# Offset and mask projections in 64x64 TensorE tiles, and convolution statistics as ScalarE sums, in a four-layer convolution kernel

## The chip, the cores and the metric

One core of a Trainium2 chip runs the whole program as one launch. The metric is device microseconds from start to end of that launch, lower being better. The core has five engines that run their own instruction streams side by side: TensorE (PE, matrix multiplies into PSUM), VectorE (DVE), ScalarE (ACT), GpSimd (POOL) and SyncE (SP, which here only issues DMAs). PE has a second row in the profile, PEld, for loading the stationary operand of a multiply. All data is float32, and each float32 matrix multiply of the program appears as two MATMUL instructions in the profile.

## The reference

The input x is 8 images of 128 channels and 96x96 pixels. Four residual layers follow each other, each preceded by a group normalization. Only layer 0 is touched by the change:

```python
x1 = lax.conv_general_dilated(x, dw_w, window_strides=(1, 1), padding=[(1, 1), (1, 1)], feature_group_count=C, ...)
x1 = x1 + dw_b[None, :, None, None]
mu = jnp.mean(x1, axis=(1, 2, 3), keepdims=True)
var = jnp.var(x1, axis=(1, 2, 3), keepdims=True)
x1 = (x1 - mu) * lax.rsqrt(var + GN_EPS)
x1 = x1 * gn_w[None, :, None, None] + gn_b[None, :, None, None]
x1 = jax.nn.gelu(x1, approximate=False)
om = jnp.einsum('nhwc,oc->nhwo', jnp.transpose(x1, (0, 2, 3, 1)), om_w) + om_b
...
offs = om[..., :2 * K2].reshape(N, H, W, G, K2, 2)
mask = om[..., 2 * K2:]
...
samp = gather(y0i, x0i) * ((1 - ly) * (1 - lx))[..., None] + gather(y0i, x0i + 1) * ((1 - ly) * lx)[..., None] + ...
out = jnp.sum(samp * mask[..., None], axis=4)
...
x = x + _L0_conv_ref(_gn(x), ...)
x = x + _L1_conv_ref(_gn(x), L1_conv_kernel)
x = x + _L2_conv_ref(_gn(x), L2_conv_weight, L2_conv_alpha_x, L2_conv_alpha_w)
x = x + _L3_conv_ref(_gn(x), L3_conv_kernel, L3_conv_bias)
```

Layer 0 is a deformable convolution. A depthwise 3x3 convolution, normalized over the whole image and passed through GELU, is projected by a 128-channel matrix onto 216 values for each pixel: a horizontal offset, a vertical offset and a mask for each of 72 taps (8 groups of 9). The image is then sampled bilinearly at the displaced places.

## The kernel before

The program has three stages in time: layer 0, then layers 1 and 2 together, then layer 3. Layer 0 works on chunks. An image is split into two bands of 48 rows, and chunk c of 12 holds four rows of each band, so 96 chunks in all. Two layouts are in use. In the plain layout a partition is one of 128 channels, and the free axis holds the two bands (2 x 384). In the band layout a partition is a band and one of 64 channels, and the free axis holds the two halves of the channels (2 x 384). The normalized image `xq` is in band layout.

For each image, `image` computes the statistics and the normalization, and then the depthwise convolution: nine taps for each chunk (`tap`, L568), each of four 64x64 multiplies whose stationary operands are diagonal matrices. Its input is in band layout and its result in plain layout. ACT moves the result out of PSUM (L588), DVE takes statistics with two `bn_stats` (L596), and SP stores it to DRAM as `x1d`. For the first image only, four of the twelve chunks are convolved by DVE (L560, L562) with the result in band layout. At the end of an image `bn_aggr` (L628), `mid1` and `end1` make the scale and bias of the following GELU.

`chunk` then does the sampling. SP loads the stored convolution in plain layout (L655), ACT applies GELU (L660), and `project` (L666) makes the three projections, vertical, mask and horizontal, each as two 128x128 multiplies with 384 columns. ACT turns the offsets into tent weights h (L679, L669, L692), DVE multiplies the mask in (L721), POOL multiplies vertical by horizontal weights to `wt` (L764, nine per chunk). For each of 25 shifts PE selects and sums the taps (`select`, L774, four 64x64 multiplies), and DVE multiplies the selected weights by the shifted image (L791). The 25 products of a chunk are added up by one of three engines, as a letter for each says: P by POOL (L809), D by DVE (L798), E by PE as four multiplies with an identity (L751). ACT moves the sum out (L817) and SP stores it (L820).

PSUM has three buffers `w` for the selects, projections, convolutions and small statistics, and one buffer `s` for the sums. There are three `wt` buffers and five `pr` buffers for products.

The order of instructions is fixed when the program is built. `Plan` is given tasks with an engine, a cost, dependencies, buffers and a priority, and steps through them: a free engine takes the ready task of lowest priority value whose buffers are free. The constants `STEP`, `OM_SLOT`, `WT_AHEAD`, `ADD_LAG`, `DW_SLOT` and `DW_PACE` make the priorities. The costs only set the order; on the chip the engines wait for each other by semaphores.

Of the kernel before, what the change touches and what calls it, by code (L numbers as in the profile page):

```python
# [11 lines left out]
F32 = mybir.dt.float32  # L12
I32 = mybir.dt.int32
AF = mybir.ActivationFunctionType
# [53 lines left out]
ADDERS = ("PPEDEPEPEPPDEEPEDPEDPEPPD", "PPPEEDPEPPEDDEEPPPEDEEPED")  # L68
LAST_ADDERS = "EDEPPEEDPEEDPEEEDPPEPEEPD"
# [5 lines left out]
WT_AHEAD = 6.3  # L75
ADD_LAG = 660.8
DW_SLOT = 2.2
DW_PACE = 1.1
# [122 lines left out]
def kernel(  # L201
# [35 lines left out]
    def half(j):  # L237
        return slice(j * HC, (j + 1) * HC)
# [154 lines left out]
    with ExitStack() as ph:  # L393
# [7 lines left out]
        omq = wp.tile([P, 3, P], F32, name="omq")  # L401
# [5 lines left out]
        dwbq = wp.tile([P, NB], F32, name="dwbq")  # L407
        for j in range(NB):
            rows = slice(j * HC, j * HC + GR)
            taps = slice(j * GR, (j + 1) * GR)  # L410
            nc.scalar.dma_start(sel[rows, :, :], c_sel[taps, :, half(j)])
            nc.scalar.dma_start(shift[rows, :], c_shift[taps, :])
            with nc.allow_non_contiguous_dma(reason="216 biases, one per partition"):
                nc.scalar.dma_start(omb[rows, :], om_b[:, taps].rearrange("k r -> r k"))
            for k in range(3):
                nc.scalar.dma_start(omq[:, k, rows], om_wT[:, k * GK + j * GR : k * GK + (j + 1) * GR])
            nc.scalar.dma_start(dwq[half(j), :, :], dw_w.rearrange("(j c) t -> c j t", c=HC))
            with nc.allow_non_contiguous_dma(reason="128 biases"):
                nc.scalar.dma_start(dwbq[half(j), :], dw_b.rearrange("(j c) o -> c (j o)", c=HC))
        dwd = wp.tile([P, NB, K2, HC], F32, name="dwd")  # L420
# [13 lines left out]
        for name, n, psum in (  # L434
            ("w", 3, True), ("s", 1, True), ("pr", 5, False), ("acc", 2, False), ("acc2", 2, False),
            ("y", 2, False), ("wt", 3, False), ("h0", 2 * NR, False), ("h1", 2 * NR, False),
            ("o", 2, False), ("x1c", 2, False), ("x1", 2, False), ("junk", 1, False),
        ):
            if psum:
                tiles = [pp.tile([P, CB, 512], F32, name=f"ps_{name}{k}") for k in range(n)]  # L440
            else:
                tiles = [wp.tile([P, NB, FB], F32, name=f"{name}_{k}") for k in range(n)]
            plan.pool(name, tiles, in_order=name != "w")
# [19 lines left out]
        for i in range(2):  # L463
            smalls.append({
                name: wp.tile([P, n], F32, name=f"{name}{i}")
                for name, n in (
                    ("st", NB * NST * 6), ("mv", 2 * NB), ("mean", NB), ("d", NB), ("sd", NB), ("sc", NB), ("bi", NB),
                    ("st1", NST * NB * 6), ("mv1", 2), ("mean1", 1), ("v1", 1), ("sd1", 1), ("sc1", 1), ("bi1", 1),
# [3 lines left out]
        def image(i, at):  # L472
# [73 lines left out]
            st1 = small["st1"][:].rearrange("p (a b) -> p a b", b=6)  # L546
            outs, stats1 = [], []
            for c in range(NST):
# [28 lines left out]
                for t in range(K2):  # L577
# [5 lines left out]
                    else:  # L583
# [4 lines left out]
                    lambda x1=x1, ps=ps, bias=None if on_dve else dwb[:]: nc.scalar.activation(  # L588
                        x1.tile[:], ps.tile[:, :, :FB], AF.Identity, **({} if bias is None else {"bias": bias})
# [3 lines left out]
                for b in range(NB):  # L593
                    stats1.append(plan.task(
                        "DVE", 0.49,
                        lambda b=b, c=c, x1=x1: nc.vector.bn_stats(st1[:, c * NB + b, :], x1.tile[:, b, :]),  # L596
                        [ev], when + 8, uses=[x1],
                    ))
# [47 lines left out]
            t = plan.task("DVE", 0.7, lambda: end1(b4.tile), [t], when, uses=[b4])  # L646
# [3 lines left out]
        def chunk(i, c, at, made):  # L650
# [3 lines left out]
            ld = plan.task(  # L654
                "SP", 0.64, lambda: nc.sync.dma_start(x1.tile[:], band_rows(x1d[i], c)),  # L655
                [outs[c]], at - STEP - 10, uses=[x1], lag=3.0,
            )
            ge = plan.task(
                "ACT", 0.95,
                lambda: nc.scalar.activation(x1.tile[:], x1.tile[:], AF.Gelu, bias=bi1[:], scale=sc1[:]),  # L660
                [ld, coefs1], at - STEP, uses=[x1],
            )

            def project(k, ps):
                for b in range(NB):
                    nc.tensor.matmul(ps[:, b, :FB], omq[:, k, :], x1.tile[:, b, :], start=True, stop=True)  # L666
# [6 lines left out]
            for k in (1, 0):  # L673
                ps, o = plan.buf("w"), plan.buf("o")
                when = at - STEP + (0.5 if k == 1 else OM_SLOT)
                t = plan.task("PE", 1.6, lambda k=k, ps=ps: project(k, ps.tile), [ge], when, uses=[ps, x1, o])
# [33 lines left out]
                if k == 1:  # L710
                    pm = plan.buf("w")
                    t = plan.task(
                        "PE", 1.6, lambda pm=pm: project(2, pm.tile),
# [107 lines left out]

        neg1 = wp.tile([P, 1], F32, name="neg1")
# [827 lines left out]
```

## Time and profile before

| | us |
|---|---|
| three runs | 5731.64, 5794.74, 5796.0 |
| their median | 5794.74 |
| profiled execution, its own time | 5726.59 |
| its span, first to last instruction | 5724.6 |
| first and last select of layer 0 (L774) | 142.7 and 3507.8 |
| first multiply of layer 1 (L1157) | 3562.1 |
| first multiply of layer 3 (L1561) | 4964.2 |
| mean granted TensorE clock | 0.988 of full |

The first number of a row in a view of windows is the stretch in us from the start of the span, then its length, and for each engine the time it was busy in it and, in brackets, the instructions that began in it. In a timeline a row has the start, the length, the engine, the line of the source, the operation, output and inputs, and how many instructions were merged into the row. In a row of a group the mean of one instruction is in ns after the total in us; after the bar stands the idle time of the engine just before those instructions, and what ended most of it. The three runs and the profiled execution lie at two places, near 5730 and near 5795.

### The profile page before, as it was taken

The page shows a single profiled execution, that of the slowest core. Times are in us where ns is not written, and L with a number is a line of the kernel's source. Part 1 is how long each engine was busy: PE and PEld are TensorE (multiplying, and loading weights), DVE is VectorE, ACT ScalarE, POOL GpSimd, SP SyncE. Part 2 cuts the span into 40 slices and gives each one's busy share as a digit, 9 for nine tenths or more (in the row PEclk, how much of TensorE's full clock was granted, in tenths as well). Part 3 has the DMA queues.
Part 4 walks back from the last instruction along what each step waited for, and adds up shares of the span by engine and source line. Part 5 has one row for each costly group of instructions (what it writes and reads, how often), then busy time and mean ns, then how long its engine had stood idle before and what let it go on. Part 6 is the DMA issues. An engine that isn't in the chain of part 4 may idle for free. (4 is left out here: it accounts for less than half of the span.)

```text
span 5724.6 us, 121348 instructions
## 1 busy us (share of the span) xinstructions
PE 5466.1 (95%) x49697; PEld 2948.3 (52%) x49697; DVE 4982.4 (87%) x7139; ACT 3131.3 (55%) x4141; POOL 4535.9 (79%) x2830
## 2 busy tenths in 40 slices
PE   4999999999999999999999996999999999899999
PEld 2444444444444444444444443544444444599999
DVE  6889889889889889889888997789999988788887
ACT  3655555555555655655655552467877776533333
POOL 0999999999999999999999996699999998322222
PEclk9999999999999999999999998999999999999999
DMA  5111111211211211211111113323333321233232
GB/s 123 50 57 57 55 57 57 57 57 57 58 57 57 58 57 57 55 59 57 48 48 46 43 40 88 104 76 87 95 96 98 90 65 48 75 105 102 98 111 78
DMA packets 434625, 397.81 MB, mean 69 GB/s; under 512 B 248976, under 2 KB 421520, under 8 KB 434064
## 3 DMA queue, kind: packets, MB, share of 16 engines
q1 hardware_dynamic: 403872, 351.23, 21.7%
q10 hardware_dynamic: 30192, 38.75, 1.9%
q8 instruction: 395, 6.47, 0.5%
q14 instruction: 166, 1.36, 0.1%
HBM read 238.90 MB, written 150.99 MB: 68 GB/s over the span
## 5 line engine op out<-in xcount | busy, mean ns | idle before, releaser
L774 PE MATMUL ps_w<-wt,sel 64*64 64x384 f32 x19200 | 1850.8, 488 | 47.1 <-ACT x L588 14.3
L791 DVE TENSOR_TENSOR pr<-ps_w,xq 128x768 f32<-128x768 f32 x1824 | 1675.3, 949 | 252.5 <-PE ps_w L774 201.9
L809 POOL TENSOR_TENSOR acc<-acc,pr 128x768 f32<-128x768 f32 x882 | 1614.0, 1837 | 194.8 <-DVE pr L791 193.3
L764 POOL TENSOR_TENSOR wt<-h,h 128x768 f32<-128x768 f32 x864 | 1578.0, 1837 | 191.3 <-ACT h L692 137.7
L774 PEld LDWEIGHTS ps_w<-wt,sel 64*64 64x64 f32 x19200 | 698.9, 132 | 967.5 <-issue 475.2
L1157 PE MATMUL ps_C<-dC,km 128*128 128x384 f32 x2304 | 768.3, 490 | 21.1 <-POOL dC L1145 9.6
L751 PE MATMUL ps_s<-pr,idq 64*64 64x384 f32 x7536 | 754.6, 484 | 0.4 <-ACT y L817 0.4
L679 ACT ACTIVATE o<-ps_w,omb 128x768 f32<-128x768 f32 x192 | 172.8, 900 | 1022.6 <-PE ps_w L666 948.3
L1285 DVE SCALAR_TENSOR_TENSOR ps_C<-xqC,w2s,ps_C 128x768 f32<-128x768 f32 x660 | 664.8, 1012 | 22.3 <-POOL xqC L1247 11.3
L1501 POOL TENSOR_TENSOR xtD<-xtD,cr 128x384 f32<-128x384 f32 x192 | 192.1, 1001 | 601.7 <-ACT cr L1500 601.7
L568 PE MATMUL ps_w<-xq,dwd 64*64 64x384 f32 x6624 | 630.4, 488 | 13.5 <-ACT x L588 10.3
L1157 PEld LDWEIGHTS ps_C<-dC,km 128*128 128x128 f32 x2304 | 429.3, 189 | 358.4 <-issue 38.6
L669 ACT ACTIVATE h<-o,shift 128x768 f32<-128x768 f32 x576 | 533.0, 925 | 12.2 <-ACT o L679 0.7
L791 DVE TENSOR_TENSOR ps_w<-ps_w,xq 128x768 f32<-128x768 f32 x480 | 458.8, 956 | 50.3 <-PE ps_w L774 50.1
L692 ACT ACTIVATE h<-h 128x768 f32<-128x768 f32 x576 | 486.3, 844 | 17.5
L666 PE MATMUL ps_w<-x1c,omq 128*128 128x384 f32 x1152 | 450.3, 514 | 16.6 <-DVE pr L791 11.3
L1302 POOL TENSOR_TENSOR ptC<-ptC,ptC 128x768 f32<-128x768 f32 x252 | 464.8, 1845 | 0.2
L798 DVE TENSOR_TENSOR acc<-ps_w,acc 128x768 f32<-128x768 f32 x480 | 455.7, 949 | 6.0
L751 PEld LDWEIGHTS ps_s<-pr,idq 64*64 64x64 f32 x7536 | 292.5, 133 | 313.7 <-issue 268.4
L1145 POOL TENSOR_TENSOR dC<-ywC 128x392 f32<-128x392 f32 x384 | 359.9, 972 | 98.3 <-PE ps_C L1157 53.6
L1561 PE MATMUL ps_b<-tr,km 128*128 128x192 f32 x2304 | 407.5, 325 | 14.4 <-DVE tr L1546 14.4
L568 PEld LDWEIGHTS ps_w<-xq,dwd 64*64 64x64 f32 x6624 | 258.2, 133 | 302.2 <-issue 229.7
(180 smaller groups left out, 7087.3 us busy)
## 6 DMA issues: line engine op xcount, KB each, us to landing
ywC<-y SPq DMA_DIRECT2D x80, 480.0 KB, 3.9
x1c<-x1d SPq DMA_DIRECT2D x96, 384.0 KB, 3.6
acc<-in_x SPq DMA_DIRECT2D x192, 192.0 KB, 3.3
y<-y SPq DMA_DIRECT2D x96, 384.0 KB, 3.2
ysC<-y SPq DMA_DIRECT2D x96, 384.0 KB, 3.3
x<-oC SPq DMA_DIRECT2D x192, 192.0 KB, 2.7
xtD<-x SPq DMA_DIRECT2D x24, 1536.0 KB, 7.1
out<-xtD ACTq DMA_DIRECT2D x24, 1536.0 KB, 5.7
```

Source lines behind the costliest of these rows:

```text
L568: nc.tensor.matmul(ps.tile[half(j), b, :FB], dwd[half(b), j, t, :], xq[half(b), r0 : r0 + RB, j, c0 : c0 + W], start=(t == 0), stop=(t == ...
L669: nc.scalar.activation(h, o, AF.Abs, bias=shift[:, k * NR + r : k * NR + r + 1])
L692: lambda h=h: nc.scalar.activation(h.tile[:], h.tile[:], AF.Relu, bias=1.0, scale=-1.0),
L751: nc.tensor.matmul(total.tile[half(j), b, :FB], idq[half(b), :], pr.tile[half(b), j, :], start=first, stop=last)
L764: lambda wt=wt, hy=hy, hx=hx: nc.gpsimd.tensor_tensor(wt.tile[:], hy.tile[:], hx.tile[:], ALU.mult),
L774: nc.tensor.matmul(ps.tile[half(b), j, :FB], sel[half(j), n, :], wt.tile[half(j), b, :], start=True, stop=True)
L791: nc.vector.tensor_tensor(view(pr.tile), view(ps.tile), x_s, ALU.mult)
L798: lambda ps=ps: nc.vector.tensor_tensor(acc.tile[:], ps.tile[:, :, :FB], acc.tile[:], ALU.add),
L809: lambda pr=pr, acc2=acc2: nc.gpsimd.tensor_tensor(acc2.tile[:], acc2.tile[:], pr.tile[:], ALU.add),
L1157: nc.tensor.matmul(ps.tile[:, b, :FB], km1[:, k, x_, :], d.tile[:, k, :, x_ : x_ + W], start=(x_ == 0), stop=(x_ == 2))
L1285: nc.vector.scalar_tensor_tensor(view, rows8(src, t), w[:, t : t + 1], view, ALU.mult, ALU.add)
L1302: lambda a=parts[0], b=pt: nc.gpsimd.tensor_tensor(a.tile[:], a.tile[:], b.tile[:], ALU.add),
```

## The change

The input of the projections is now loaded in band layout. The projection weights `omq` are arranged for 64x64 tiles, and each of the three projections is eight 64x64 multiplies, two accumulating steps over the halves of the channels with four tiles each. GELU needs a scale and bias for each half of the channels and becomes two activations of 384 columns. The load is two DMAs of 64 partitions in place of one of 128.

The statistics of the convolution come from ACT: the activation that moves the result out of PSUM also gives the sum, and a second activation squares the difference from the bias and gives its sum. Both `bn_stats` go. At the end of an image five small DVE operations take the place of `bn_aggr`, and `end1` makes a scale and a bias for both halves.

Setup loads `omq` in eight DMAs in place of six, and two vectors more, in two DMAs each. Some letters of the adders trade places: the two patterns in turn keep their counts (11 P, 9 E, 5 D and 10 P, 10 E, 5 D), and that of the last image goes from 8 P, 12 E, 5 D to 7 P, 13 E, 5 D. Four constants of the priorities and the costs given to the planner change. Layers 1 to 3 are not touched.

```diff
-ADDERS = ("PPEDEPEPEPPDEEPEDPEDPEPPD", "PPPEEDPEPPEDDEEPPPEDEEPED")
-LAST_ADDERS = "EDEPPEEDPEEDPEEEDPPEPEEPD"
+ADDERS = ("PPEDEPEPEPPDEEPDEPEDPEPPD", "PPPEEDPEPPEDDEEEPPEDPEPED")
+LAST_ADDERS = "EDEEEEPDPEEDPEEEDPPEPEPED"
...
-WT_AHEAD = 6.3
-ADD_LAG = 660.8
-DW_SLOT = 2.2
-DW_PACE = 1.1
+WT_AHEAD = 6.45
+ADD_LAG = 1048.6
+DW_SLOT = 2.21
+DW_PACE = 4.76
...
-        omq = wp.tile([P, 3, P], F32, name="omq")
+        omq = wp.tile([P, NB, 3, P], F32, name="omq")
...
-            for k in range(3):
-                nc.scalar.dma_start(omq[:, k, rows], om_wT[:, k * GK + j * GR : k * GK + (j + 1) * GR])
+            for b in range(NB):
+                for m in range(NB):
+                    nc.scalar.dma_start(
+                        omq[half(b), j, :, m * HC : m * HC + GR],
+                        om_wT[half(j), :].rearrange("c (k r) -> c k r", k=3)[:, :, m * GR : (m + 1) * GR],
+                    )
...
+                nc.scalar.dma_start(gnwq[half(j), :], gn_w.rearrange("(j c) o -> c (j o)", c=HC))
+                nc.scalar.dma_start(gnbq[half(j), :], gn_b.rearrange("(j c) o -> c (j o)", c=HC))
...
                     "ACT", 0.9,
-                    lambda x1=x1, ps=ps, bias=None if on_dve else dwb[:]: nc.scalar.activation(
-                        x1.tile[:], ps.tile[:, :, :FB], AF.Identity, **({} if bias is None else {"bias": bias})
+                    lambda c=c, x1=x1, ps=ps, bias=None if on_dve else dwb[:]: nc.scalar.activation(
+                        x1.tile[:], ps.tile[:, :, :FB], AF.Identity, **({} if bias is None else {"bias": bias}),
+                        accum_out=st1[:, 0, c : c + 1],
                     ),
                     prev, when + 6, uses=[ps, x1],
                 )
-                for b in range(NB):
-                    stats1.append(plan.task(
-                        "DVE", 0.49,
-                        lambda b=b, c=c, x1=x1: nc.vector.bn_stats(st1[:, c * NB + b, :], x1.tile[:, b, :]),
-                        [ev], when + 8, uses=[x1],
-                    ))
+                jk = plan.buf("junk")
+                stats1.append(plan.task(
+                    "ACT", 0.9,
+                    lambda c=c, x1=x1, jk=jk: nc.scalar.activation(
+                        jk.tile[:], x1.tile[:], AF.Square, bias=ndwb[:], accum_out=st1[:, 1, c : c + 1]
+                    ),
+                    [ev], when + 8, uses=[x1, jk],
+                ))
...
-                nc.vector.tensor_scalar(r, r, gnw[:], None, ALU.mult)
-                nc.vector.tensor_copy(sc1[:], r)
-                nc.vector.tensor_scalar(r, r, mean1[:], -1.0, ALU.mult, ALU.mult)
-                nc.vector.tensor_scalar(bi1[:], r, gnb[:], None, ALU.add)
+                for j in range(NB):
+                    q = ps[:, 1, 1 + j : 2 + j]
+                    nc.vector.tensor_scalar(q, r, gnwq[:, j : j + 1], None, ALU.mult)
+                    nc.vector.tensor_copy(sc1[:, j : j + 1], q)
+                    nc.vector.tensor_scalar(q, q, mean1[:], -1.0, ALU.mult, ALU.mult)
+                    nc.vector.tensor_scalar(bi1[:, j : j + 1], q, gnbq[:, j : j + 1], None, ALU.add)
...
-            t = plan.task(
-                "DVE", 0.8, lambda: nc.vector.bn_aggr(mv1[:], small["st1"][:]), stats1, when
-            )
+            def aggr1():
+
+                d1, n = small["d1"], NST * NB * FB
+                nc.vector.tensor_reduce(d1[:], st1, AX.X, ALU.add)
+                nc.vector.tensor_scalar(mv1[:], d1[:], 1.0 / n, None, ALU.mult)
+                nc.vector.tensor_scalar(d1[:, 0:1], mv1[:, 0:1], dwb[:], None, ALU.subtract)
+                nc.vector.tensor_scalar(d1[:, 1:2], d1[:, 0:1], d1[:, 0:1], -1.0, ALU.mult, ALU.mult)
+                nc.vector.tensor_scalar(mv1[:, 1:2], mv1[:, 1:2], d1[:, 1:2], None, ALU.add)
+
+            t = plan.task("DVE", 0.8, aggr1, stats1, when)
...
-                "SP", 0.64, lambda: nc.sync.dma_start(x1.tile[:], band_rows(x1d[i], c)),
+            def load_x1():
+                for b in range(NB):
+                    f0 = b * HB * W + c * FB
+                    nc.sync.dma_start(
+                        x1.tile[half(b), :, :], x1d[i].rearrange("(j c) f -> c j f", c=HC)[:, :, f0 : f0 + FB]
+                    )
...
-                lambda: nc.scalar.activation(x1.tile[:], x1.tile[:], AF.Gelu, bias=bi1[:], scale=sc1[:]),
+            def gelu():
+                for j in range(NB):
+                    rows = x1.tile[:, j, :]
+                    nc.scalar.activation(rows, rows, AF.Gelu, bias=bi1[:, j : j + 1], scale=sc1[:, j : j + 1])
...
             def project(k, ps):
-                for b in range(NB):
-                    nc.tensor.matmul(ps[:, b, :FB], omq[:, k, :], x1.tile[:, b, :], start=True, stop=True)
+
+                for j in range(NB):
+                    for m in range(NB):
+                        for b in range(NB):
+                            nc.tensor.matmul(
+                                ps[half(m), b, :FB],
+                                omq[half(b), j, k, half(m)],
+                                x1.tile[half(b), j, :],
+                                start=(j == 0),
+                                stop=(j == NB - 1),
+                            )
...
-                t = plan.task("PE", 1.6, lambda k=k, ps=ps: project(k, ps.tile), [ge], when, uses=[ps, x1, o])
+                t = plan.task("PE", 1.29, lambda k=k, ps=ps: project(k, ps.tile), [ge], when, uses=[ps, x1, o])
```

More of the change, by code (lines that the diff above doesn't have):

```diff
@@ L407 @@
         dwbq = wp.tile([P, NB], F32, name="dwbq")
+        gnwq = wp.tile([P, NB], F32, name="gnwq")
+        gnbq = wp.tile([P, NB], F32, name="gnbq")
         for j in range(NB):
@@ L414 @@
                 nc.scalar.dma_start(omb[rows, :], om_b[:, taps].rearrange("k r -> r k"))
-            for k in range(3):
-                nc.scalar.dma_start(omq[:, k, rows], om_wT[:, k * GK + j * GR : k * GK + (j + 1) * GR])
+            for b in range(NB):
[4 more added lines that the diff above has]
+                    )
             nc.scalar.dma_start(dwq[half(j), :, :], dw_w.rearrange("(j c) t -> c j t", c=HC))
-            with nc.allow_non_contiguous_dma(reason="128 biases"):
+            with nc.allow_non_contiguous_dma(reason="128 values of each"):
                 nc.scalar.dma_start(dwbq[half(j), :], dw_b.rearrange("(j c) o -> c (j o)", c=HC))
+                nc.scalar.dma_start(gnwq[half(j), :], gn_w.rearrange("(j c) o -> c (j o)", c=HC))
+                nc.scalar.dma_start(gnbq[half(j), :], gn_b.rearrange("(j c) o -> c (j o)", c=HC))
         dwd = wp.tile([P, NB, K2, HC], F32, name="dwd")
@@ L442 @@
                 tiles = [wp.tile([P, NB, FB], F32, name=f"{name}_{k}") for k in range(n)]
-            plan.pool(name, tiles, in_order=name != "w")
+            plan.pool(name, tiles, in_order=name not in ("w", "junk"))
         def load_rows(i, lo, hi):
@@ L467 @@
                     ("st", NB * NST * 6), ("mv", 2 * NB), ("mean", NB), ("d", NB), ("sd", NB), ("sc", NB), ("bi", NB),
-                    ("st1", NST * NB * 6), ("mv1", 2), ("mean1", 1), ("v1", 1), ("sd1", 1), ("sc1", 1), ("bi1", 1),
+                    ("st1", 2 * NST), ("mv1", 2), ("d1", 2), ("mean1", 1), ("v1", 1), ("sd1", 1), ("sc1", NB), ("bi1", NB),
                 )
@@ L544, in image @@
                 ))
-            st1 = small["st1"][:].rearrange("p (a b) -> p a b", b=6)
+            st1 = small["st1"][:].rearrange("p (k c) -> p k c", k=2)
             outs, stats1 = [], []
@@ L645, in image @@
             )
-            t = plan.task("DVE", 0.7, lambda: end1(b4.tile), [t], when, uses=[b4])
+            t = plan.task("DVE", 1.2, lambda: end1(b4.tile), [t], when, uses=[b4])
             return outs, t, sc1, bi1
@@ L653, in chunk @@
             x1 = plan.buf("x1c")
-            ld = plan.task(
-                "SP", 0.64, lambda: nc.sync.dma_start(x1.tile[:], band_rows(x1d[i], c)),
[L656 to L662, printed above, removed]
-            def project(k, ps):
-                for b in range(NB):
-                    nc.tensor.matmul(ps[:, b, :FB], omq[:, k, :], x1.tile[:, b, :], start=True, stop=True)
+            def load_x1():
[8 more added lines that the diff above has]
+                    nc.scalar.activation(rows, rows, AF.Gelu, bias=bi1[:, j : j + 1], scale=sc1[:, j : j + 1])
+            ld = plan.task("SP", 1.2, load_x1, [outs[c]], at - STEP - 10, uses=[x1], lag=3.0)
+            ge = plan.task("ACT", 1.15, gelu, [ld, coefs1], at - STEP, uses=[x1])
+            def project(k, ps):
+                for j in range(NB):
[8 more added lines that the diff above has]
+                            )
             def absolute(h, o, k, r):
@@ L712, in chunk @@
                     t = plan.task(
-                        "PE", 1.6, lambda pm=pm: project(2, pm.tile),
+                        "PE", 1.29, lambda pm=pm: project(2, pm.tile),
                         [ge] + [tent[1, r][0] for r in RES_ORDER], when + 5, uses=[pm, x1],
@@ L820, in chunk @@
             plan.task("SP", 0.56, lambda: nc.sync.dma_start(band_rows(y1[i], c), y.tile[:]), [ev], at + STEP, uses=[y], lag=2.5)
+        ndwb = wp.tile([P, 1], F32, name="ndwb")
+        nc.vector.tensor_scalar(ndwb[:], dwb[:], -1.0, None, ALU.mult)
         neg1 = wp.tile([P, 1], F32, name="neg1")
```

## The prediction

> **What bounds the kernel now.** I read the page first: its busy shares, the slices and the chain that ended last. The chain goes back only to 3521.78 us, where the loads of layers 1 and 2 begin; layer 0 ends before that, so the stage the change touches must be read from its own windows.
>
> ```profile
> PE   4999999999999999999999996999999999899999
> DVE  6889889889889889889888997789999988788887
> POOL 0999999999999999999999996699999998322222
> ```
>
> Up to slice 24 (3.4 ms) PE and POOL are both at nine tenths and DVE close behind. The small dips of DVE repeat, once for each image. So I cut one image into windows. The sum of a chunk leaves ACT (L817) at 1048, 1378 and 1479 us after nine and three more chunks; the other images repeat this to within 2 us. The third row is the last image.
>
> ```profile
> core 0: us, PE busy (x) PEld busy (x) DVE busy (x) ACT busy (x) POOL busy (x), PEclk, DMA share, GB/s
> 1048.00:1378.00 330.00, 326.32 (x3560) 147.84 (x3556) 287.39 (x341) 169.41 (x219) 299.09 (x168) 1.00 0.19 57
> 1378.00:1479.00 101.00, 95.36 (x984) 41.16 (x980) 95.02 (x127) 70.11 (x95) 98.12 (x56) 1.00 0.21 56
> 3187.00:3512.00 325.00, 323.18 (x3488) 143.59 (x3484) 313.32 (x354) 164.52 (x212) 307.84 (x172) 1.00 0.12 36
> ```
>
> The reader is to see two regimes. In nine chunks of twelve, while PE also makes the next image's convolution, PE is busy 98.9% and POOL 90.6%: PE sets the pace. In the other three there is no convolution, POOL is busy 97.1% and PE 94.4%: POOL sets the pace. In the last image PE (99.4%), DVE (96.4%) and POOL (94.7%) are close together.
>
> **The change part by part.** *Projections, 57 us gained.* The timeline of PE shows one among 64x64 work:
>
> ```profile
> 163.81 2.14 PE L774 MATMUL ps_w<-wt,sel 64*64 64x384 f32 x24
> 165.75 1.50 PE L751 MATMUL ps_s<-pr,idq 64*64 64x384 f32 x16
> ...
> 173.14 0.82 PE L774 MATMUL ps_w<-wt,sel 64*64 64x384 f32 x8
> 173.89 1.56 PE L666 MATMUL ps_w<-x1c,omq 128*128 128x384 f32 x4
> 175.38 0.88 PE L774 MATMUL ps_w<-wt,sel 64*64 64x384 f32 x8
> ```
>
> Starts count, as lengths overlap. Eight 64x64 instructions take (165.75-163.81)/3 = 0.647 us. From 173.14 to 175.38 are 2.24 us for eight of them and one projection, which so costs 1.59: 1.49 of its own and 0.10 before it can start. As 16 instructions of 64x64 it will cost 2 x 0.647 = 1.29. Gain 0.30.
>
> Here two statements of the Trainium skill meet this row. "TensorEngine Tiling (Array Packing)", section The Problem, has the full array underused where a dimension is at most 64. These projections contract 128 channels into 108 columns: by that rule there is nothing to gain, and the sum would lose these 57 us. Its Key Properties say that a change of tiling mode drains the array; by that only the 0.10 goes, 0.10 x 3 x 63 = 19 us. The rows decide: beyond the entry, four full-array instructions take 1.49 us against 1.29 for sixteen small ones with the same multiplications. Accumulating twice into one bank is covered by the convolution, which adds nine taps in 64x64 tiles (L568, 488 ns mean, as L774's 488).
>
> It counts only where PE sets the pace: 27 projections in nine chunks, seven images, 7 x 27 x 0.30 = 57 us. POOL and DVE allow it: 330-8 leaves POOL at 299/322 = 93%, below the 97% it reaches elsewhere. In the POOL-bound three chunks I count nothing, since the adders keep their counts: 0, with bounds of 10 us either way for the altered order.
>
> *Statistics off DVE, 14 us gained.* These rows price them and what replaces them:
>
> ```profile
> L596 DVE BATCH_NORM_STATS2 st<-x 128x6 f32<-128x384 f32 x192 | 100.4, 549 | 22.6 <-ACT x L588 22.6
> L705 ACT ACTIVATE junk<-junk,neg 128x768 f32<-128x768 f32 x192 | 179.5, 935 | 5.6
> L705 ACT ACTIVATION_READ_ACCUMULATOR junk<-junk,neg 128x1 f32 x192 | 35.9, 187 | 0.0
> L537 ACT ACTIVATE xq<-xq,bi,sc 128x384 f32<-128x384 f32 x192 | 121.4, 698 | 0.1
> L660 ACT ACTIVATE x1c<-x1c,bi,sc 128x768 f32<-128x768 f32 x96 | 96.7, 1015 | 0.2
> POOL wt L764 <- DVE st L596: 18.2, 6, 3.3
> PEld ps_w L666 <- DVE st L596: 8.4, 14, 0.6
> ```
>
> DVE loses 24 x 0.549 = 12.6 us in the nine chunks of an image, where it is not the limit. Only waits that ended with it count: 18.2 + 8.4 us in all. I take about half, 2 us an image, 14; ends 0 and 30.
>
> *More on ACT, nothing.* A convolution chunk adds a Square with its accumulator read (935+187 ns, as L705) and one more read, 1.3 us; GELU in halves adds 2 x 0.70 - 1.01 = 0.4. No table load is added in the built instruction order. ACT goes from 169 of 330 us to about 188 of 322 (12 x 1.3 + 9 x 0.4 more), 58%: its idle time covers it. Uncovered it would be 96 x 1.7 = 163 us. Queued behind a Square are the moves of projections out of PSUM (L679), for which PE's next buffer waits.
>
> *Small operations at an image's end.* Five reductions and scalings for one `bn_aggr` (0.8 us) and four more in `end1` add some 1.3 us on DVE by the 0.2 to 0.28 us of such operations; they fall in the POOL-bound three chunks, with DVE at 94%. I leave them inside that part's bounds.
>
> *DMAs.* The split load adds one issue, 0.7 us by the two of the residual (1.29) against one of 0.56, on SP. Behind it stand loads of the next image and the store of y. "DMA: Bandwidth & Descriptors", Rules for kernel authors, calls halves in two DMAs not worth it, as both use the same engines. By that rule it is pure cost, at most 96 x 0.7 = 67 us if every issue were late. The rows price less: 192 KB of the residual land in 3.3 us, 384 KB of x1 in 3.6, DMA engines are at 19%, and SP issues some 6 us in 36. Nothing. The six added setup issues on ACT's queue (0.34 to 0.7 us each, 3 us) end near 26 us, before ACT's first work at 47.9; the statistics of x, still loading until 42, cover them. Uncovered: 3 us.
>
> *Start, 13 us gained.* From 50 to 117 us DVE is busy 62.1 us, of which 22 `bn_stats` of L596 are 10.9, and the convolution by DVE makes PE wait. Against it the tail grows: Square and read (1.1) for a `bn_stats` (0.55), 1.3 us of small operations, GELU halves, and normalizations that the new order puts before the first GELU. I take 5 us, ends 0 and 10. The new order also puts two of the second image's convolution chunks (18 taps, 11.6 us) before the first select, into idle time of PE:
>
> ```profile
> 127.21 7.94 PE L666 MATMUL ps_w<-x1c,omq 128*128 128x384 f32 x16 [4.41 <-ACT x1c L660]
> 142.69 6.08 PE L774 MATMUL ps_w<-wt,sel 64*64 64x384 f32 x48 [7.54 <-POOL wt L764]
> ```
>
> That relieves PE in the first chunks until POOL limits them: 8 us, ends 4 and 11. How long a convolution holds one of three PSUM buffers is unaltered, though `DW_PACE` grows: on average 4.8 selects stand between its first and last tap, 5.0 before.
>
> *Last image, 3 us gained.* PE loses 0.90 and takes one more addition (0.65) a chunk, POOL one fewer. DVE at 96.4% is late next: 3, ends 0 and 8.
>
> **Sum:** 57+14+13+3 = 87 us in layer 0; the other layers stay.
>
> **Against which time.** The sum is made in an execution of 5726.59 us (span 5724.6). The median of the runs is 5794.74, 68 higher: of four known executions two lie near 5730, two near 5795, and the trace does not show why. I set the forecast between, 5761 - 87 = 5674 us; on the lower level it is 5640, on the upper 5708.
>
> **The rivals.** *Waits take it.* With PE quicker, POOL's products and DVE's releases of PSUM become late in the nine chunks also; 30 us remain, mostly the start: 5731. For: three engines near 90% with three buffers each. Against: POOL stands at 90.6% there and has shown 97%.
>
> *Stalls go too.* Shorter projections hold PSUM less long and DVE is freer, so PE's waits (L666 alone waits 98.3 us for DVE products, on its weight row) shrink, and the POOL-bound part gains: 140 us, 5621. For: the planner's cost for a projection now equals the chip's. Against: in those chunks PE idles only 3.7 of 330 us.
>
> *Slower: ACT comes late.* If the Square stands before the move of a projection, PE lacks a buffer. At 1.7 us a chunk fully exposed, 163 - 87 = 76 us slower: 5837; it decides from 55% exposure. For: ACT moves all PSUM results but the products. Against: ACT idles 49% there, and PE's waits for L588 sum to tens of us only. Slower by 2% needs about 2.1 us of new waits a chunk.
>
> *It doesn't do what it says:* four tiles that run one after another would need over 2.6 us a projection. The rows of L568 exclude it.
>
> **How the numbers follow.** Chances: the sum above 62%, own range of gain 60 to 115; stalls too 20%; waits take it 13%; ACT late 5%. 2% is 116 us from the median, so 5679, about what a measurement of this kernel can tell from no change. The first case passes that on the lower level (half of 62%) and with 4% on the upper, the second nearly always (20%): faster 0.55. The rest is within 2%, 0.42, and slower keeps 0.03. The range: the second case on the lower level gives 5587 and the third on the upper 5765; leaving out a tenth at either end, 5600 to 5738.
>
> **What would show it.** Projections of 1.29 us from start to start with no entry gap; the nine chunks near 320 us with PE at 98%, the three still near 100 with POOL at 97%; first select near 137; ACT below 60%. Wrong would be PE below 96% in the nine chunks, or waits of PE for L679 or the Square of more than 50 us.

## The result and the profile after

The changed kernel's median is 5703.81 us (20 runs, 5697.09 to 5769.25) against 5794.97 for the kernel before on the same chip (20 runs, 5725.57 to 5797.87). The ratio is 0.9887 with a 95% interval of 0.9854 to 0.9919, within 2% of no change. The profiled execution took 5701.26 us, with a span of 5699.2; the forecast was 5674.

The 91 us between the medians are of two kinds. Both kernels have two levels, 65 to 69 us apart: of these 20 runs the kernel before had 5 on its lower level (near 5727) and the changed one 17 on its own (near 5703). On equal levels the change is worth only some 25 us. The experiments take both parts up.

The slices of the page after, for the three engines shown before:

```profile
PE   5899999999999999999999996999999999899999
DVE  5888889889889889889888997789999988788887
POOL 0899999999999999999999985699999998322222
```

The only lasting difference is that DVE has come down slightly. The windows of the changed kernel follow: nine chunks and the three after them, cut as before by sums leaving ACT, then the last image, and then one whole image (the third). A row has start, length, and busy time and instruction starts of each engine.

```profile
core 0: us, PE busy (x) PEld busy (x) DVE busy (x) ACT busy (x) POOL busy (x), PEclk, DMA share, GB/s
1046.00:1360.00 314.00, 309.83 (x3776) 154.61 (x3772) 270.72 (x309) 180.34 (x254) 293.48 (x165) 1.00 0.20 61
1360.00:1470.00 110.00, 102.87 (x1184) 43.98 (x1180) 102.39 (x143) 74.20 (x106) 103.57 (x59) 1.00 0.18 50
3159.00:3484.00 325.00, 322.76 (x3920) 161.70 (x3912) 313.20 (x354) 165.57 (x221) 287.85 (x161) 1.00 0.11 36
1006.00:1430.20 424.20, 412.90 (x4952) 198.61 (x4952) 373.09 (x451) 254.75 (x358) 396.88 (x223) 1.00 0.19 58
```

The nine chunks fell by 16 us and the three rose by 9. Part of this is only work that moved across the cut: POOL began 168 instructions in the nine before and 165 now, 56 and 59 in the three. So the whole image must be read. The same image of the kernel before:

```profile
1008.00:1438.70 430.70, 421.99 (x4520) 188.92 (x4520) 381.24 (x467) 238.46 (x310) 396.75 (x223) 1.00 0.20 57
```

Before, 36 projections at 1.59 us and 4376 small multiplies at 1.29/16 us make 410 us of work for PE, and 21 us of 430.7 are lost to late starts. After, 4952 small multiplies make 399, and 25 are lost. PE's work fell by 11 us, this image by 6.5. The rest came back as late starts. Part of them show as idle time of PE: these rows give, over the six images after the first, what PE waited for products of DVE before a select, first in the kernel before, then in the changed one (us in total, times, longest).

```profile
PE ps_w L774 <- DVE pr L791: 11.0, 21, 0.9
PE ps_w L810 <- DVE pr L827: 24.9, 40, 1.9
```

By stages, the last sum of layer 0 leaves ACT at 3483.8 us, before at 3512.3: 28.5 earlier. The end of the first image comes 2.5 us *later* (579.8 against 577.3), the six images after it take 424.8 each on average in place of 430.0 (31 us in all), and the last takes 355.3 in place of 354.8. From the first multiply of layer 1 to that of layer 3 are 2.8 us more than before, and layer 3 is unaltered in these two executions (760.4 us).

The timeline of PE and ACT in the changed kernel near its start:

```profile
118.35 7.14 PE L576 MATMUL ps_w<-xq,dwd 64*64 64x384 f32 x56
...
129.14 6.06 PE L576 MATMUL ps_w<-xq,dwd 64*64 64x384 f32 x72
...
144.15 0.88 PE L810 MATMUL ps_w<-wt,sel 64*64 64x384 f32 x8 [1.11 <-ACT o L715]
146.17 0.88 PE L810 MATMUL ps_w<-wt,sel 64*64 64x384 f32 x8 [1.14 <-DVE acc L827]
148.12 0.88 PE L810 MATMUL ps_w<-wt,sel 64*64 64x384 f32 x8 [1.08 <-DVE pr L827]
...
158.15 0.88 ACT L596 ACTIVATE x<-ps_w,dwb 128x768 f32<-128x768 f32 x1
...
164.43 0.89 ACT L596 ACTIVATE x<-ps_w,dwb 128x768 f32<-128x768 f32 x1
...
170.41 1.46 PE L696 MATMUL ps_w<-x1c,omq 64*64 64x384 f32 x16
171.70 3.02 PE L810 MATMUL ps_w<-wt,sel 64*64 64x384 f32 x32
```

The last two rows price a projection: 171.70-170.41 = 1.29 us, with no entry before it. The rows above them show what the start costs. The taps of the second image's first two chunks are done by 135, but ACT moves their results out of PSUM at 158 and 164: ACT works almost without a pause from 127 on, and tent weights and normalizations stand ahead of the first move in its order. Till then two of three PSUM buffers are taken, and selects go one at a time, 2 us apart, most of them waiting for the product of the last. The first sum leaves ACT at 198.1 us, before at 185.8.

### The profile page after: what moved, and what is told of

Same layout as the page of the kernel before. It is cut to its first block, busy times and chain, and to the rows that moved or that the text cites. A ratio compares the mean times of both kernels' runs of the same rounds, so it can differ in the third digit from the quotient of the medians.

```text
span 5699.2 us, 129079 instructions
## 1 busy us (share of the span) xinstructions
PE 5414.1 (95%) x53249; PEld 3037.7 (53%) x53249; DVE 4916.1 (86%) x7012; ACT 3262.2 (57%) x4525; POOL 4518.7 (79%) x2818
## 5 line engine op out<-in xcount | busy, mean ns | idle before, releaser
L810 PE MATMUL ps_w<-wt,sel 64*64 64x384 f32 x19200 | 1870.7, 488 | 76.2 <-DVE pr L827 34.4
L845 POOL TENSOR_TENSOR acc<-acc,pr 128x768 f32<-128x768 f32 x870 | 1595.6, 1844 | 146.4 <-DVE pr L827 144.6
L810 PEld LDWEIGHTS ps_w<-wt,sel 64*64 64x64 f32 x19200 | 746.1, 132 | 950.1 <-issue 256.3
L787 PE MATMUL ps_s<-pr,idq 64*64 64x384 f32 x7632 | 774.9, 484 | 2.0 <-ACT y L853 2.0
L787 PEld LDWEIGHTS ps_s<-pr,idq 64*64 64x64 f32 x7632 | 324.6, 133 | 293.9 <-issue 121.3
L696 PE MATMUL ps_w<-x1c,omq 64*64 64x384 f32 x4608 | 431.6, 487 | 11.0 <-DVE pr L827 6.8
L1183 POOL TENSOR_TENSOR dC<-ywC 128x392 f32<-128x392 f32 x384 | 359.8, 970 | 98.7 <-PE ps_C L1195 54.1
L576 PEld LDWEIGHTS ps_w<-xq,dwd 64*64 64x64 f32 x6624 | 280.0, 133 | 273.3 <-issue 115.2
```

Of the source, the lines that this page charges most:

```text
L576: nc.tensor.matmul(ps.tile[half(j), b, :FB], dwd[half(b), j, t, :], xq[half(b), r0 : r0 + RB, j, c0 : c0 + W], start=(t == 0), stop=(t == ...
L787: nc.tensor.matmul(total.tile[half(j), b, :FB], idq[half(b), :], pr.tile[half(b), j, :], start=first, stop=last)
L810: nc.tensor.matmul(ps.tile[half(b), j, :FB], sel[half(j), n, :], wt.tile[half(j), b, :], start=True, stop=True)
L845: lambda pr=pr, acc2=acc2: nc.gpsimd.tensor_tensor(acc2.tile[:], acc2.tile[:], pr.tile[:], ALU.add),
```

## The experiments

The changed kernel is taken apart first, then the two levels, then the waits that came back.

**The kernel before, once more** (no edit).

> The kernel before, unchanged, for a second profile. Of twenty runs of it five lie near 5727 us and fifteen near 5796; its first profile was one of the lower ones, at 5726.6. If the 68 us lie in one stage, a profile near 5796 shows that stage longer and the rest alike to within a few us: theory A has layer 0 identical (its last select near 3508 us) and the extra time in layers 1 to 3; theory B has it spread over all stages in proportion (1.2%), as a slower clock would. If the profile falls near 5727 again, nothing is decided.

Of 12 runs 6 lay on either level (5727 to 5797). In its profile layer 0 ends at 3512.3 us, as before. The levels need no edit.

**The second image's convolution held back** until the ninth product of chunk 0:

```diff
+                held = muls[0, 0][HOLD : HOLD + 1] if i == 1 else []
...
-    "PE", 0.645, lambda t=t, tap=tap: tap(t), need + prev, when + DW_PACE * t,
+    "PE", 0.645, lambda t=t, tap=tap: tap(t), need + held + prev, when + DW_PACE * t,
```

> The changed kernel, with the convolution of the second image held back until the ninth product of the first chunk. Theory (two early convolution chunks occupy two of three PSUM buffers until ACT moves them out at 158 and 164 us, so selects run one at a time): selects of chunk 0 follow each other at about 0.9 us instead of 1.96, the first sum leaves ACT (L853) near 186 us instead of 198, and the end of layer 0 comes 8 to 13 us earlier than the 3483.8 us of the changed kernel. Rival (POOL's products limit the first chunk, and the early convolution is a real saving of PE work): the end of layer 0 is the same or up to 10 us later.

The median is 5687.6 us (5682.10 to 5755.15, 20 runs). The timeline of its PE, where the first selects now run together:

```profile
122.57 7.37 PE L698 MATMUL ps_w<-x1c,omq 64*64 64x384 f32 x64 [5.17 <-ACT x1c L688]
137.98 6.97 PE L812 MATMUL ps_w<-wt,sel 64*64 64x384 f32 x48 [8.04 <-POOL wt L802]
```

The first sum comes at 181.4 us, and layer 0 ends at 3467.0, 16.8 earlier than in the changed kernel, more than the theory had said. 13.4 of it is there at the end of the first image (566.4 against 579.8); the six images after it take 424.2 us each, against 424.8. The early convolution, which put PE to use while idle, was a loss, because it kept the PSUM buffers. With it out of the way the projections of the first chunk begin at 122.57, 4.6 us earlier than in the kernel before (127.21).

**One part alone.** The projections in small tiles with `bn_stats`, `bn_aggr`, letters and constants as before:

```diff
 (the changed kernel)
-                        jk.tile[:], x1.tile[:], AF.Square, bias=ndwb[:], accum_out=st1[:, 1, c : c + 1]
+                        lambda b=b, c=c, x1=x1: nc.vector.bn_stats(st1[:, c * NB + b, :], x1.tile[:, b, :]),
```

> The kernel before with the projections in 64x64 tiles alone (band load, GELU in halves); statistics by bn_stats on DVE, the old letters of the adders and the old constants. Theory (the projections are what shortens an image, and about half of their saved PE time of 11 us an image returns as waits before selects): an image takes 423 to 427 us, against 430 before and 424 to 426 after. Rival (the gain comes from DVE losing the statistics, or from the new constants): 428 us or more.

5698.20 to 5701.27 us on the lower level (3 of 4 runs), 425.7 us an image: all of the change's gain. Layer 0 ends at 3481.5, with the first sum at 186.8 us and no early convolution. The statistics by ACT alone, in the kernel before:

```diff
 (the kernel before)
-                        lambda b=b, c=c, x1=x1: nc.vector.bn_stats(st1[:, c * NB + b, :], x1.tile[:, b, :]),
+                        jk.tile[:], x1.tile[:], AF.Square, bias=ndwb[:], accum_out=st1[:, 1, c : c + 1]
```

> The kernel before with the statistics as sums by ScalarE alone; projections, letters of the adders and constants as before. Theory: DVE is not the limit, an image stays at 428 to 431 us, and at the start the end of the first image's convolution comes some 5 us earlier. Rival (DVE's releases of PSUM held PE up): 424 to 427 us.

They cost time, which neither expectation had: 5748 to 5756 us on the lower level, where the kernel before has 5725 to 5732, and 433.4 us an image against 430.0. One image in a row of windows:

```profile
1013.80:1446.50 432.70, 421.22 (x4520) 187.24 (x4520) 373.20 (x447) 251.71 (x347) 397.11 (x223) 1.00 0.19 57
```

DVE has 8 us less to do in it (373 against 381), and nothing of it shows. Here two chunks of the second image are convolved ahead of the first select again, and the first sum comes at 195.5 us.

Does the Square hold up ACT? In the same program, with the order of PE, POOL and SP the same, it was cut to two columns:

```diff
-                        jk.tile[:], x1.tile[:], AF.Square, bias=ndwb[:], accum_out=st1[:, 1, c : c + 1]
+                        jk.tile[:, 0, :2], x1.tile[:, 0, :2], AF.Square, bias=ndwb[:], accum_out=st1[:, 1, c : c + 1]
...
-                nc.vector.tensor_scalar(mv1[:, 1:2], mv1[:, 1:2], d1[:, 1:2], None, ALU.add)
+                nc.vector.tensor_scalar(mv1[:, 1:2], mv1[:, 1:2], 0.0, 16.0, ALU.mult, ALU.add)
```

> The kernel before with the new statistics alone, in the same order on every engine, but the Square treats two columns in place of 768 and the variance is set to a constant; so its 0.94 us become some 0.25, 0.7 us less ScalarE in each of 96 chunks. Theory (the statistics alone cost 23 us because the Square stands ahead of moves out of PSUM on ScalarE): the image returns from 433 us to 430 or below, 5715 to 5730 us on the lower level. Rival (the order that the planner made for it costs the 23 us, whatever ScalarE's time): 432.5 to 434 an image, 5745 to 5757 us.

The group of the Square in this kernel (it was 936 ns with 768 columns):

```profile
L597 ACT ACTIVATE junk<-x,ndwb 128x2 f32<-128x2 f32 x96 | 28.3, 295 | 2.9
```

The image stays at 433.3 us and the lower level at 5748 to 5756. The length of the Square is not the cause. The order that the planner makes once the tasks differ is what remains as the likely one; it was not isolated.

Then the changed kernel with letters and constants of before:

```diff
-WT_AHEAD = 6.45
-ADD_LAG = 1048.6
-DW_SLOT = 2.21
-DW_PACE = 4.76
+WT_AHEAD = 6.3
+ADD_LAG = 660.8
+DW_SLOT = 2.2
+DW_PACE = 1.1
```

> The changed kernel with the letters of the adders and the four constants of the priorities as before. If the parts add up (projections alone gain 26 us, the statistics alone cost 23 us), both with the old order stand near the kernel before: 427 to 430 us for an image, 5715 to 5727 us on the lower level, and the new letters and constants are what gives the 23 back. Rival (projections and statistics help each other, the new constants do little): 424 to 426 us for an image and 5697 to 5705.

5697.08 to 5702.71 us on the lower level (4 of 5 runs), 424.9 us an image. The rival held: the parts don't add up. The statistics cost 23 us beside the old projections and nothing in sum beside the new ones, and the letters and constants do nothing that can be measured. That nothing has two halves: against the projections alone the end of the first image comes 7.0 us later (580.3 against 573.4), and the six images after it take 0.8 us less each. The early convolution stands in this kernel too, with the first sum at 198.9 us, so it came with the statistics and not with the new constants.

**The two levels.** The statistics' profile fell on the upper level (span 5816.3 us), and there layer 3 takes 828.0 us against 760.4; all else is as usual. Three more profiles fell there (of the kernels with the cut Square, with the old letters and constants, and with GpSimd's additions halved), with 828.2 to 828.9 us in layer 3; the ten on the lower level have 759.9 to 760.5. The two windows are 400 us of layer 3, first in that kernel, then in the kernel before:

```profile
5088.30:5488.30 400.00, 377.52 (x2256) 364.99 (x2255) 382.58 (x657) 125.20 (x281) 101.16 (x94) 1.00 0.28 95
```

```profile
5064.20:5464.20 400.00, 400.00 (x2463) 400.00 (x2462) 336.44 (x718) 136.65 (x307) 102.10 (x103) 1.00 0.30 103
```

On the lower level PE never pauses. On the upper one DVE is busier (383 us) with fewer instructions, so one of them takes longer. The timeline of DVE, ACT and POOL, upper level first:

```profile
5289.77 0.52 ACT L1512 ACTIVATE cr<-y 128x384 f32<-128x384 f32 x1
5290.04 0.58 DVE L1558 TENSOR_TENSOR tr<-row 128x408 f32<-128x408 f32 x1
...
5290.37 1.12 POOL L1513 TENSOR_TENSOR xtD<-xtD,cr 128x384 f32<-128x384 f32 x1 [3.63 <-ACT cr L1512]
5290.54 1.38 DVE L1559 TENSOR_TENSOR tr<-row 128x408 f32<-128x408 f32 x1
...
5294.27 1.00 POOL L1513 TENSOR_TENSOR xtD<-xtD,cr 128x384 f32<-128x384 f32 x1 [2.78 <-ACT cr L1512]
5294.30 1.41 DVE L1558 TENSOR_TENSOR tr<-row 128x408 f32<-128x408 f32 x1
```

```profile
5265.42 0.52 ACT L1500 ACTIVATE cr<-y 128x384 f32<-128x384 f32 x1
5265.48 0.58 DVE L1548 TENSOR_TENSOR tr<-row 128x408 f32<-128x408 f32 x1
...
5265.98 0.35 DVE L1484 TENSOR_TENSOR pq<-ps_b,m 128x192 f32<-128x192 f32 x1
5266.01 1.00 POOL L1501 TENSOR_TENSOR xtD<-xtD,cr 128x384 f32<-128x384 f32 x1 [2.90 <-ACT cr L1500]
5266.25 0.35 DVE L1485 TENSOR_TENSOR pq<-ps_b,m 128x192 f32<-128x192 f32 x1
```

In the slow pace GpSimd's addition starts just ahead of a sum or difference of two SBUF operands on VectorE, and that operation takes 1.38 to 1.41 us instead of 0.58, ending 0.43 us after GpSimd (5290.54+1.38 against 5290.37+1.12). In the fast pace it lies beside operations of which one operand is in PSUM, and nothing is lengthened. The four upper traces have this all through layer 3: in some 760 us of it 179 of these sums and differences take over 1 us in each trace, every one of them starts during an addition of GpSimd, and every one ends 0.43 to 0.46 us after it. In six traces of the lower level (the kernel before and the changed one, with and without the gate that follows, among them) none starts there and none takes over 1 us. The Trainium skill, "SBUF — State Buffer", section SBUF: two separate sides, fits this: the two engines share a port pair as an exclusive lock, which a VectorE operation with two SBUF inputs needs beside a GpSimd operation that reads SBUF, and the later one is blocked fully. The measured end, 0.43 us after GpSimd and not 0.58, leaves 0.15 us of the operation that GpSimd did not hold up. Why a run keeps its pace is read from the order and not tested: GpSimd starts after ACT's ReLU, which stands behind a move that waits for PE, and in the slow pace PE waits for VectorE. Layer 3 works on 192 half rows, so the loss is (828.0-760.4)/192 = 0.35 us for each.

The gate puts GpSimd's start behind VectorE's second difference, and ReLU and normalization ahead of the move:

```diff
             cr = sp.tile([P, b - a, W], F32, name="cr")
+            if gate:
+                nc.vector.memset(cr[:, 0, 0:1], 0.0)
             nc.scalar.activation(cr[:], y[:], AF.Relu)
...
                 nc.vector.tensor_tensor(tm[:], at(h, 1), at(h, 0), ALU.subtract)
+                if late:
+                    add_out(gate=True)
                 nc.vector.tensor_tensor(ta[:], at(h, 0), at(h, 2), ALU.subtract)
...
                 state[h] = pa, pb, m2
-                if late:
-                    add_out()
```

> The kernel before, with one change in layer 3: GpSimd's addition of a finished half row (1.00 us) may only start after VectorE has made the second of its three differences, by a one-column memset in the input of the ReLU, and that ReLU and the normalization stand ahead of the move of m2 on ScalarE. Nothing of layers 0 to 2 is touched. Theory (the two levels come from that addition lying either beside operations of VectorE that read PSUM, or beside one of its additions of two SBUF operands, which then take 1.38 us in place of 0.58): the upper level near 5795 vanishes, all executions lie within 10 us of each other near 5727, and layer 3 takes 758 to 765 us. Rival (the levels have another cause, such as the clock or the memory): executions still fall on two levels some 68 us apart, about as often as before.

All 20 runs lie between 5726.81 and 5732.28 us, while the kernel before, run beside it, spread over both levels (24 of 39 on the lower). The timeline of the gated kernel:

```profile
5266.70 0.06 DVE L1501 MEMSET cr<- 128x1 f32 x1
5266.81 0.53 ACT L1502 ACTIVATE cr<-y 128x384 f32<-128x384 f32 x1
5267.17 0.35 DVE L1484 TENSOR_TENSOR pq<-ps_b,m 128x192 f32<-128x192 f32 x1
...
5267.41 1.00 POOL L1503 TENSOR_TENSOR xtD<-xtD,cr 128x384 f32<-128x384 f32 x1 [2.83 <-ACT cr L1502]
```

GpSimd now always meets the operations on PSUM, no operation is lengthened, and the upper level is gone: the cause of the levels is shown. The gate has two parts, the memset and the earlier place of the ReLU and the normalization (with a load) on their engines; which of them is needed was not tried apart. The same edit on the changed kernel:

> The changed kernel with the same change to layer 3. Theory: one level only, near 5699, so that the change itself, free of the levels, is worth 25 to 28 us against the gated kernel before. Rival: two levels, 5700 and 5768, remain.

5701.88 to 5705.12 us (4 runs). Gate against gate the change is worth 5728.62-5703.13 = 25.5 us, 0.45%. The rest of the 91 was which level the runs fell on. That is not all chance: over all runs ungated kernels with the new projections were on the lower level in 62 of 77, the kernel before in 69 of 150 and the two with the statistics alone in 25 of 40. How layer 0 sets the odds was not tried.

**The waits that came back.** Each of the next three shortens one kind of operation in the changed kernel to half of its columns, with the order kept, and so leaves half of those sums or products out of the output. First GpSimd's additions:

```diff
-nc.gpsimd.tensor_tensor(acc2.tile[:], acc2.tile[:], pr.tile[:], ALU.add)
+nc.gpsimd.tensor_tensor(acc2.tile[:, 0], acc2.tile[:, 0], pr.tile[:, 0], ALU.add)
```

> The changed kernel, where GpSimd adds only the first half of the columns of each of its products to its sum (the other half is left out of the output), with the same order of instructions on every engine; this takes some 0.9 us from each of about 9 additions of a chunk, 8 us of GpSimd's 33. Theory (the waits of TensorE that came back, 23 us an image, come from GpSimd being late, first with the products that the selects need): the image falls from 424 us to 405 to 412 with TensorE's work unchanged at 401, 85 to 130 us in all. Rival (they come from VectorE and ScalarE giving PSUM buffers back, three of them in turn): less than 4 us an image, under 30 us in all.

Then VectorE's additions to its own sum, with the products for them:

```diff
+                        k = 1 if pr is ps else NB
-                        nc.vector.tensor_tensor(view(pr.tile), view(ps.tile), x_s, ALU.mult)
+                        nc.vector.tensor_tensor(view(pr.tile)[:, :k], view(ps.tile)[:, :k], x_s[:, :k], ALU.mult)
...
-                            lambda ps=ps: nc.vector.tensor_tensor(acc.tile[:], ps.tile[:, :, :FB], acc.tile[:], ALU.add),
+                            lambda ps=ps: nc.vector.tensor_tensor(acc.tile[:, 0], ps.tile[:, 0, :FB], acc.tile[:, 0], ALU.add),
```

> The changed kernel, where each of VectorE's five additions of a chunk, and the product made for it in place, treats half of the columns (the other half is left out of the sum), in the same order on every engine: ten operations of 0.95 us become ten of some 0.55, 4 us less VectorE in a chunk, 48 us an image of its 348. Theory (the 23 us of waits an image are PSUM buffers that VectorE gives back late): the image falls from 424 to 408 to 416, 55 to 110 us in all. Rival (TensorE would wait as long for ScalarE, for GpSimd or for its own order of work): less than 3 us an image, under 20 us in all.

Last the other products, with buffers zeroed at the start:

```diff
+                        k = NB if pr is ps else 1
-                        nc.vector.tensor_tensor(view(pr.tile), view(ps.tile), x_s, ALU.mult)
+                        nc.vector.tensor_tensor(view(pr.tile)[:, :k], view(ps.tile)[:, :k], x_s[:, :k], ALU.mult)
```

> The changed kernel, where each of VectorE's 20 products of a chunk for TensorE's and GpSimd's sums treats half of the columns (the other half of the product buffers stays zero and is left out of the output), in the same order on every engine; 20 operations of 0.95 us become 20 of some 0.55, 8 us less VectorE in a chunk, twice what the halved additions took away, and this time in the operation that gives a PSUM buffer back after a select. Theory (what is left of TensorE's waits is the ring of three PSUM buffers, a select needing the product of the third select before it, so that places where selects follow each other run at the pace of products): the image falls from 424 us to 402 to 412, 90 to 160 us in all. Rival (the waits go around, as with the halved additions and with GpSimd's halved sums, each wait removed being replaced by another): 418 to 423 us an image.

One row each, the third image's window in this order:

```profile
1009.00:1435.50 426.50, 414.17 (x4952) 199.75 (x4952) 374.82 (x451) 254.70 (x358) 306.18 (x222) 1.00 0.19 58
```

```profile
996.40:1418.80 422.40, 411.94 (x4952) 203.13 (x4952) 330.75 (x451) 254.71 (x359) 396.87 (x223) 1.00 0.20 58
```

```profile
985.30:1401.00 415.70, 407.22 (x4956) 210.36 (x4952) 290.08 (x451) 254.72 (x358) 396.76 (x223) 1.00 0.20 59
```

GpSimd with 91 us less to do (306 against 397) shortens nothing: 5708 to 5718 us on the lower level, above the changed kernel. It is not the limit, though busy 94% of the image; that theory fell. VectorE's additions, 42 us less, give 2.5 us an image and 24 in all, the second a little more than the rival had allowed. The products, 83 us less, give 8.7 us an image, and 5634.89 us to 5637.9 on the lower level: between the two expectations. So of PE's 25 us of late starts about a third hangs on the length of these products. A product frees a PSUM buffer after a select, feeds the sums and takes VectorE's time; the run does not part the three. The other 17 remain even then, and their cause stays open.

**Both repairs together**, the held convolution and the gate on the changed kernel (the two edits above):

> Both repairs on top of the change: the second image's convolution waits for a product of chunk 0 (worth 17 us alone) and GpSimd's addition in layer 3 waits for VectorE's second difference. Theory: they add up; one level, 5680 to 5690 us, 13 to 20 below the changed kernel with the second repair alone (5703), and 0.982 of the kernel before by the medians of all runs or lower. Rival: the runs fall on two levels again, or the gated layer 3 loses what the held convolution gains and the median stays at 5700.

5686.43 to 5688.87 us (4 runs), median 5687.78. That is 15.4 us below the gated change and 40.8 below the gated kernel before, on one level. The ratio to the median of before, expected at 0.982 or lower, was 0.993, as the kernel before, run beside it, had most of its runs (15 of 23) on the lower level. It is the best complete version found, by its typical time and by its lack of an upper level.

## Why the prediction was right, and where it was not

*The size.* The median lies 30 us above the forecast, inside the range, and within 2%, to which 0.42 was given; 0.55 had gone to more. But that it came so near is luck. The sum said 87 us in layer 0, and the trace and the gated pair show 28.5 and 25.5. Level against level the forecast missed by some 60 us: 5640 was said for the lower one, where the median is 5703, and 5708 for the upper one, where the three runs lie at 5767 to 5769. The kernel before ran mostly on its upper level and the changed one mostly on its lower, and that shift, which nobody had forecast, filled the gap. By its size this is the rival "waits take it" (30 us), which was right in part about DVE, but it put most of the 30 into the start, which gave none, and made POOL late, which it is not.

*Projections, 57.* The price was right to the hundredth (1.29 us, no entry gap), and PE's work fell by 11 us an image. The failing step is "It counts only where PE sets the pace", with PE's 98.9% busy as the evidence. PE's busy time hid late starts in small pieces: in an image of the kernel before, PE is busy 422.0 us for 410 us of work, with 8.7 us idle besides. With the shorter projections 21 us of late starts became 25, and of some 10 us that the parts for projections and statistics promise for an image 5 came, 31 us in six images. That the next select then meets its wait sooner is a reading and not shown; the waits for products (11.0 us before, 24.9 after) speak for it. The skill's "TensorEngine Tiling (Array Packing)", section PSUM Bottleneck, warns that tiling speeds TensorE but not the emptying of PSUM. The run with halved products points the same way, with a third of the late starts, though it does not single out PSUM. Of the step's other half, "POOL and DVE allow it", POOL's holds by experiment and DVE's only in part.

*Statistics off DVE, 14.* Nothing beside the new projections, and minus 23 alone. The step took half of the waits that ended with `bn_stats`. That such a wait ended with an instruction did not mean that it would go with it: with `bn_stats` gone the image alone became 3.4 us longer. The cover for ACT was argued rightly: the Square's length costs nothing (433.3 against 433.4 us an image), and ACT is at 60%. Less than nothing was excluded by the ends "0 and 30", without a reason, and that was the error.

*Start, 13.* It was a loss of 2.5. The failing step is "How long a convolution holds one of three PSUM buffers is unaltered": the count of selects between first and last tap says nothing of the time until ACT takes the result out, some 30 us after the last tap here. The first select came at 144, not 137. The 8 us for early convolutions have the wrong sign: holding them back gained 17. The other 5 us were about right: with the convolution held, the first projection begins 4.6 us earlier than before.

*Last image, 3.* Minus 0.5. DVE, named as late next, is at 96.4% as before.

*Setup DMAs, split loads, small operations.* Counted at nothing. The kernel with the projections alone, which has the split loads and the GELU halves, shows all of the gain; they were not isolated.

*Against which time.* The forecast was set between the levels because "the trace does not show why". It was visible with a second trace only: layer 3's VectorE and GpSimd. "The other layers stay" missed that a change in layer 0 can go with other odds for the pace of layer 3.

*What would show it.* Nine chunks of 314 us with PE at 98.7% (near 320 and 98 said), three of 110 with POOL at 94% (near 100 and 97 said), together 424 against 420. These signs were nearly met while the sum was 59 us too large: the four or five us an image, and the loss at the start, had no sign in them but the first select.

## What to carry to other kernels

Where three engines are above 85%, as here, an engine's busy share did not tell what shortening its work was worth: count its late starts in one period, and allow for their growth. Halving one kind of operation with the order kept tells in one run whether an engine is the limit; GpSimd at 94% was not. When runs of one kernel fall on two levels, compare traces from both levels, stage by stage, before a difference of medians is credited to a change.

## What was not expected of the hardware

A VectorE addition of two SBUF operands took 1.38 us in place of 0.58 when GpSimd had started 0.17 us before it, and this phase held through all of layer 3, with 68 us lost; a memset of 0.06 us on the way of GpSimd's input, with the ReLU and the normalization moved ahead on ACT, kept it away in 28 of 28 gated runs. Cutting GpSimd's additions to half made the kernel some 12 us slower (5715.67 against 5703.81 by the medians). 8.9 of it are in layer 0, of which 6.5 fall into the six images after the first, 1.1 in the eleventh chunk of each (40.9 us against 39.8): there the small multiply of the statistics (L654) waits for a product for 6.2 us over these images, against 1.4. Why that product is late the trace does not show. The accumulator's read is a second ACT instruction of 0.19 us whatever the columns, so a two-column Square still took 0.30+0.19 us.
